# Routing on column tiles, paired output gates, and rows turned by one VectorE transpose and 16 DMAs

## The chip, the cores and the metric

The kernel runs on one core of a Trainium2 chip. The metric is the device time of one execution in microseconds (us). PE is TensorE (with its weight loads, PEld, beside the matmuls), DVE is VectorE, ACT is ScalarE, POOL is GpSimd, SP is SyncE, which issues most DMAs.

## The reference

Two Flamingo-like layers over 16 batches of 256 tokens of width 256, all in float32:

```python
x = x + tanh(g_xattn[0]) * L0_xattn(ctx, layernorm(x))          # 16 heads of 64, keys from ctx and x
x = x + tanh(g_ffn[0]) * L0_ffn(layernorm(x))                   # 8 experts, top 2 by softmax(x @ router_w.T)
x = x + tanh(g_xattn[1]) * L1_xattn(layernorm(x), ctx, ctx, ..) # 16 heads of 16, 77 keys
x = x + tanh(g_ffn[1]) * L1_ffn(layernorm(x), ..)               # gated linear attention, below

# L1_ffn: 8 heads of 64; q1, k1, v projections; a second pair q2, k2 of rank 64
# and a router over 4 experts (top 1)
o = gla(q1, k1, v, gk1) + sum over experts of gla(q2 * fac, k2 * fac, v, gk2 * mask)
g = (x @ Wga @ Wgb).reshape(B, L, H, DV)                         # the output gates, rank 64
o = o * rsqrt(mean(o * o) + EPS) * norm_w
o = o * (g * sigmoid(g))
return o.reshape(B, L, H * DV) @ Wo
```

The expert layer takes, of each token, the two most probable experts; a token's place among its expert's rows is the number of earlier tokens that chose that expert.

## The kernel before

The work is staged by layer, and each stage walks the 16 batches in a pipeline that is written out by hand. Nearly every instruction is pinned to program order on its engine, so each engine is a queue in the order of the code. A float32 matmul stands in the trace as two records.

**First stage (`stage0_fast`), cross-attention.** For each batch four units `g` of four heads: `scores` (PE `sc`), exponentials on ACT, `sums` on POOL, `values` (PE `o`, on four column tiles of 32), a DVE reciprocal and product. Between units stand tables of steps (`ahead_of`, `behind_scores`, `behind_values`), which also run the routing of the expert layer for earlier batches, in class `Route`: `logits` (after unit 3; PE `rt`: the turned rows `xnT` as weights, 128x128, and the 8 router columns as moving operand), `exps`, `choose`, `weigh`, `ranks` (after unit 2; PE `rank`: a strictly triangular matrix `before` and a matrix of ones as weights, 16 columns moving), `place`, and `scatter` by indirect DMA on POOL's queue. `copied` takes `rt` and `rank` from PSUM with ACT. The expert rows in DRAM are cleared first, by `clear_rows`: 16 DMAs of 640 KB on SP, from a zeroed tile of 128x256. The routing of the last two batches ends in the next stage, that of the experts.

**Last stage (`stage3_fast`), gated linear attention.** It runs 64 units `p`, four per batch `b` (step `p % 4` is `m`, two heads each). The loop over `p` does, in this order: `masked(p-1, 1)`, `keys_queries(p+1)` (PE `kq`), `middle`, `rest`, `decays(p+1)` (PE `gq`, `gz`; ACT exponentials `ee`), `late`, `products(p, 0)` (PE `sc<-f`), `masked(p, 0)` (DVE `at<-sc,amask`), `behind_mask`, `factors(p+1)`, `by_rows`, in steps 1 and 2 `summed(p)` (PE `o<-at,v`), `second(p+1)` (PE `gq`/`gz` from `low`), `factors_second(p+1)`, `logs`, `products(p, 1)` (PE `sc<-q,k`), and in steps 0 and 3 `summed(p)`. `middle`, `rest`, `late`, `behind_mask`, `by_rows` and `logs` are tables that give, for each step, functions and the batch that they work for (an offset to `b`).

The functions that the change touches: `lows` (step 0, next batch) makes the low-rank products `low`; its rows 0 to 63 of part 1 are the output gates' input. `outgates(b, i)` (steps 0 and 3) makes half of the gates: two matmuls on rows 0 to 63 into one PSUM bank `zg`, an exponential on ACT; `outgates_end` copies `zg` on DVE to `zs`, takes log and exponential on ACT and multiplies on POOL into `gw`. `gated` (steps 1 and 3) uses `gw`. For the batch after next, `stats` (step 2) takes the moments, `norm_ahead` (step 2) writes the normed rows `xn` with ACT, and `turn_ahead` (step 3) turns them with 16 DVE transposes of 32x128 (`turned_squares`). `route_logits` (step 0, next batch) transposes `low` on PE into a bank `rt`, which DVE then reads.

PSUM in the last stage: `psu` holds `kq`, `gq`, `gz`, `o` (one bank each), `psa` one pair of banks for `sc`, and the pool behind `bank(name)`, f3ps, has two banks that all other results take in turn: in step 0 `den`, `low`, `rt`, `zg`; in step 1 `z`, `z`, `ms`; in step 2 `hT`, `both`, `proj`; in step 3 `ms`, `v`, `v`, `zg`.

Of the kernel before, what the change touches and what calls it, by code (L numbers as in the profile page):

```python
# [10 lines left out]
F32 = mybir.dt.float32  # L11
I32 = mybir.dt.int32
AF = mybir.ActivationFunctionType
ALU = mybir.AluOpType
# [3 lines left out]
P = 128  # L18
# [55 lines left out]
def layers(ctx: ExitStack, tc: tile.TileContext, t, out, check):  # L74
# [67 lines left out]
    for b in range(2, B):  # L142
        load_x(b)
    rw1 = load_w("rw1", D, 8, ws1)
    ew1 = load_w("ew1", D, 2048, ws1)
# [3 lines left out]
    if fast:  # L149
        bv, own, pmask = (w12.tile(shape, F32, tag=n, name=n) for n, shape in (  # L150
            ("bv", [P, D]), ("own", [P, 2, 32]), ("pmask", [P, 2])))
        before, offs = (ws1.tile(shape, F32, tag=n, name=n) for n, shape in (
            ("before", [P, P]), ("offs", [P, 2, 2, 8])))

        gbo = const("gbo", [P, D])
        for n, x in (("bv", bv), ("bo", gbo), ("own", own), ("pmask", pmask), ("before", before),
                     ("offs", offs)):
            nc.sync.dma_start(out=x, in_=t[n])
    else:
        brow = w12.tile([1, 2, D], F32, tag="brow", name="brow")  # L160
        nc.sync.dma_start(out=brow, in_=t["brow"])
        bmask = w12.tile([P, 4], F32, tag="bmask", name="bmask")
        nc.sync.dma_start(out=bmask, in_=t["bmask"])
# [231 lines left out]
    class Route:  # L395
# [32 lines left out]
        def logits(self, b, bank):  # L428
            ps, xnT = bank("rt"), self.xnT.pop(b)
            for i in range(2):  # L430
                for k in range(2):
                    pe.matmul(ps[:, 8 * i:8 * i + 8], xnT[:, k, i * P:(i + 1) * P], rw1[:, k, :],
                              start=k == 0, stop=k == 1)
            self.copied(b, ps[:, :16])

        def copied(self, b, ps):
            n = ps.shape[1]
            self.ps[b] = ws1.tile([P, n], F32, tag=f"copied{n}", name="copied")
            act.copy(self.ps[b], ps)

        def exps(self, b):

            z = self.ps.pop(b)[:, :16].rearrange("p (i e) -> p i e", i=2)
            mx = st.tile([P, 2], F32, tag="rmx", name="rmx")
            dve.tensor_reduce(mx, z, AX.X, ALU.max)
            e = self.e[b] = st.tile([P, 2, 8], F32, tag="re", name="re")
            dve.tensor_tensor(e, z, bc(mx, [P, 2, 8], 2), ALU.subtract)
            act.activation(e, e, AF.Exp)
# [58 lines left out]
        def ranks(self, b, bank):  # L507
            hs, h1, h2 = self.hs[b]
            ps = bank("rank")
            pe.matmul(ps[:, :16], before, hs[:, 0].rearrange("p i e -> p (i e)"), start=True, stop=True)  # L510
            pe.matmul(ps[:, 16:32], ones, hs[:, 1].rearrange("p i e -> p (i e)"), start=True, stop=True)
            self.copied(b, ps[:, :32])

        def place(self, b):

            (_, h1, h2), ps, count = self.hs.pop(b), self.ps.pop(b), check["rows"][:, b // 8]
            base = st.tile([P, 2, 2, 8], F32, tag="base", name="base")
            at = st.tile([P, 2, 2, 2, 8], F32, tag="at", name="at")
            row = st.tile([P, 2, 2, 2], F32, tag="row", name="row")
            n = st.tile([P, 2, 8], F32, tag="nth", name="nth")  # L520
            dve.tensor_tensor(n, ps[:, :16].rearrange("p (i e) -> p i e", i=2), bc(count, [P, 2, 8], 1), ALU.add)
            dve.tensor_tensor(count, count, ps[:, 24:32], ALU.add)
            dve.tensor_tensor(n[:, 1, :], n[:, 1, :], ps[:, 16:24], ALU.add)
            dve.tensor_tensor(base[:, 0], n, offs[:, 0], ALU.add)

            dve.scalar_tensor_tensor(base[:, 1], n, ROWS - 1.0, offs[:, 1], ALU.min, ALU.add)
            for k, h in enumerate((h1, h2)):
                dve.tensor_tensor(at[:, :, :, k], base, bc(h, [P, 2, 2, 8], 1), ALU.mult)
            dve.tensor_reduce(row, at, AX.X, ALU.add)
            dve.tensor_copy(self.pos[:, b], row)  # L530
# [24 lines left out]
    def clear_rows():  # L555
        zero = ws1.tile([P, D], F32, tag="zero", name="zero")
        nc.gpsimd.memset(zero, 0.0)
        n = ROWS // P
        for rows in route.rows:
            for e in range(8):  # L560
                nc.sync.dma_start(out=by_expert(rows, e),
                                  in_=bc(zero, [P, n, D], 1))

# [341 lines left out]
    def stage1():  # L905
        with ExitStack() as sx:
# [7 lines left out]
            def route(b):  # L914
# [4 lines left out]
                for i in range(2):  # L919
                    for k in range(2):  # L920
                        nc.tensor.matmul(ps[:, 8 * i:8 * i + 8], xnT[:, k, i * P:(i + 1) * P], rw1[:, k, :],
                                         start=k == 0, stop=k == 1)
# [694 lines left out]
    def stage3_fast(early_bank):  # L1617

        with ExitStack() as sx:
# [22 lines left out]

            lbg2 = w1.tile([64, 512], F32, tag="lbg2", name="lbg2")
            nc.sync.dma_start(out=lbg2, in_=t["lbg"][64:P, :])
            low2 = w1.tile([64, P], F32, tag="low2", name="low2")
# [3 lines left out]

            xn, xnT, low, lg, hT, em, am = {}, {}, {}, {}, {}, {}, {}  # L1650
            v, gw, u_, oT = {}, {}, {}, {}
# [17 lines left out]
            def norm_ahead(b):  # L1669
                xn[b] = w0.tile([P, 2, D], F32, tag="xn", name="xn")  # L1670
                normed(xn[b], xs[b], *mvs.pop(b))

# [8 lines left out]
            def turn_ahead(b):  # L1681

                xnT[b] = of(b).tile([P, 2, S], F32, tag="xnT", name="xnT")
                turned_squares(xnT[b], xn[b], range(16))

            def lows(b):
# [7 lines left out]
                dve3.tensor_copy(low[b][:, 0, :], ps[:, :S])  # L1694
                dve3.tensor_scalar(low[b][:, 1, :], ps[:, S:], vec[:, V_ONE:V_ONE + 1], None, ALU.add)
                if b > 0:
                    for r in range(0, 64, 32):
# [95 lines left out]

            def outgates(b, i):

                if i == 0:
                    gw[b] = w2.tile([P, 4, S], F32, tag="gw", name="gw")
                ps = bank("zg")
                for m in range(2):
                    matmul(ps[:, m * S:(m + 1) * S], lbg[0:64, (2 * i + m) * P:(2 * i + m + 1) * P],  # L1800
                           low[b][0:64, 1, :], start=True, stop=True)
                e = w2.tile([P, 512], F32, tag="eg", name="eg")
                act3.activation(e, ps, AF.Exp, scale=-1.0)
                z_[b, i] = ps, e

            def outgates_end(b, i):
                ps, e = z_.pop((b, i))
                zs = w2.tile([P, 512], F32, tag="zs", name="zs")
                dve3.tensor_copy(zs, ps)
                act3.activation(e, e, AF.Ln, bias=1.0)  # L1810
                act3.activation(e, e, AF.Exp, scale=-1.0)
                pool3.tensor_tensor(gw[b][:, 2 * i:2 * i + 2, :].rearrange("p m s -> p (m s)"), zs, e, ALU.mult)

# [121 lines left out]
            def squares(b, mp):  # L1935
                if mp == 0:
                    u_[b] = w2.tile([P, 4, S], F32, tag="u", name="u")
                    oT[b] = w2.tile([P, 4, S], F32, tag="oT", name="oT")
                ps = o.pop((b, mp))
# [44 lines left out]
            def warm():  # L1984

                ps = bank("warm")
                for _ in range(2):
# [6 lines left out]

            rest = {0: [(bias, 2)], 1: [(route, 1)], 2: [(steepest, 1, 0), (stats, 2)], 3: [(steepest, 1, 1), (turn_ahead, 2)]}
            late = {1: [(scaled, -1, 1)], 2: [(project, -1)], 3: [(vals, 1)]}
            behind_mask = {0: [(route_logits, 1)]}
            by_rows = {0: [(outgates, 0, 0)], 1: [(gates_end, 1)], 3: [(outgates, 0, 1)]}
            logs = {0: [(route_sums, 1), (outgates_end, 0, 0)], 1: [(gate_logs, 1, 0)], 2: [(gate_logs, 1, 1), (norm_ahead, 2)],
                    3: [(outgates_end, 0, 1)]}  # L2000

# [138 lines left out]
def _arrays(i):  # L2140
# [4 lines left out]
    def cols(v):  # L2145
# [34 lines left out]
        "wo0h": f["L0_xattn_Wo"].reshape(4, 4, 2, 32, D).transpose(0, 2, 1, 3, 4).reshape(1024, D),  # L2180
        "rw1": f["L0_ffn_router_w"].T, "ew1": f["L0_ffn_expert_weights"].transpose(1, 0, 2).reshape(D, 2048),
        "prio": np.broadcast_to(np.arange(8, 0, -1, dtype=np.float32), (P, 8)),
# [3 lines left out]
        "wq3": f["L1_ffn_Wq"], "wk3": f["L1_ffn_Wk"], "wv3": f["L1_ffn_Wv"], "wo3": f["L1_ffn_Wo"],  # L2186
        "before": (s < u) * np.float32(1),
        "offs": np.broadcast_to(np.float32([ALL_ROWS, ROWS]).reshape(2, 1, 1) * np.arange(8, dtype=np.float32), (P, 2, 2, 8)), "smask": smask, "halves": halves.astype(np.float32),
# [18 lines left out]
```

## Time and profile before

| | |
|---|---|
| median of 3 runs | 1860.68 us (1860.09 to 1863.35) |
| the profiled execution | 1860.41 us, span 1858.6 us |
| granted TensorE clock | 0.998 |
| PE, DVE, POOL, ACT busy | 99%, 66%, 55%, 46% |
| first stage (`sc`, `o`, `qk`, most of `rt` and `rank`) | to about 933 us |
| gated linear attention | from about 1213 us, in steady state from 1242 us |

In the lines below L50 is the helper that issues pinned instructions and L1635 and L1638 are the last stage's matmul and transpose helpers, so groups are told apart by the names of the tiles: `zg<-low,lbg` writes `zg` from `low` and `lbg`. A timeline's line gives start and duration in us, engine, line, operation, tiles, shape and count; in brackets the idle time before it and what ended it.

### The profile page before, as it was taken

The numbers are of one execution on the slowest core, as the hardware profiler recorded it, in microseconds if no ns is written. First come the engines' busy times: TensorE is split into PE (matmuls) and PEld (weight loads), VectorE is DVE, ScalarE is ACT, GpSimd is POOL, SyncE is SP. The second block draws the span as 40 slices with busy tenths as digits, with TensorE's granted clock in tenths as the row PEclk, the third lists the DMA queues.
The fourth block names the chain that finished last, engine by engine and source line by source line (L and its number), as shares of the span: only waits on it lengthen the run. The fifth ranks groups of instructions, "written<-read, shape, count | busy, mean of one in ns | idle before, by whom it ended". The sixth has DMA issues, their size and how long they took to land.

```text
span 1858.6 us, 34765 instructions
## 1 busy us (share of the span) xinstructions
PE 1833.0 (99%) x13678; PEld 1270.8 (68%) x13678; DVE 1231.4 (66%) x2903; ACT 863.9 (46%) x1804; POOL 1016.0 (55%) x1001
## 2 busy tenths in 40 slices
PE   8999999999999999999999999999999999999997
PEld 5666666666766667666777766667777777777775
DVE  3345656556655656555465388878888888888874
ACT  4433344343443434434343487845544545454542
POOL 4654767567666576656634767314444444444443
PEclk9999999999999999999999999999999999999999
DMA  9500010000010000000068933100000000000000
GB/s 322 204 3 20 18 32 15 25 16 22 24 37 7 29 20 10 28 24 19 10 213 249 250 50 48 18 1 1 12 7 7 7 12 7 7 7 7 13 7 14
DMA packets 56902, 84.62 MB, mean 46 GB/s; under 512 B 10467, under 2 KB 44371, under 8 KB 56217
## 3 DMA queue, kind: packets, MB, share of 16 engines
q1 hardware_dynamic: 44441, 65.52, 10.7%
q0 software_dynamic: 12288, 16.79, 4.5%
q8 instruction: 110, 1.80, 0.4%
q14 instruction: 63, 0.52, 0.1%
HBM read 44.00 MB, written 38.29 MB: 44 GB/s over the span
## 4 chain that ended last, share of the span: by engine, by line
PE 94%; DVE 2%; ACT 1%; POOL 1%; issue 1%; DMA 0%; SPq 0%; POOLq 0%; DVEq 0%; ACTq 0%
PE o L50 14%; PE qk L50 13%; PE sc L50 11%; PE v L50 9%; PE proj L50 7%; PE kq L1635 7%; PE sc L1635 5%; PE gq L1635 3%; PE ex L50 3%; PE v L1635 3%; PE proj L1635 3%; PE o L1635 3%; PE gz L1635 2%; PE low L1635 1%; PE ms L1635 1%; PE q L50 1%
## 5 line engine op out<-in xcount | busy, mean ns | idle before, releaser
L50 POOL TENSOR_SCALAR rs<-mv 128x2 f32<-128x2 f32 (+2 forms) x85 | 16.2, 191 | 395.4 <-DVE mv L50 393.2
L50 DVE RECIPROCAL rd<-o 128x256 f32<-128x256 f32 x64 | 112.4, 1756 | 162.6 <-PE o L50 162.6
L50 ACT ACTIVATE e<-sc 128x1024 f32<-128x1024 f32 (+1 forms) x192 | 181.5, 1015 | 18.5 <-PE sc L50 18.5
L50 PE MATMUL sc<-qk 64*128 64x256 f32 (+1 forms) x1536 | 183.1, 384 | 0.5 <-DVE qk L50 0.5
L50 PE MATMUL o<-e,v 128*32 128x256 f32 (+1 forms) x3072 | 177.9, 379 | 0.0
L50 PEld LDWEIGHTS sc<-qk 64*128 64x128 f32 (+1 forms) x1536 | 132.1, 172 | 55.0 <-issue 26.8
L50 POOL TENSOR_TENSOR esum<-esum,es 128x512 f32<-128x512 f32 x128 | 163.2, 1275 | 10.0
L50 PE MATMUL qk<-kvT,wkv 128*128 128x333 f32 x512 | 164.3, 443 | 0.0
L50 POOL TENSOR_TENSOR es<-e 128x1024 f32<-128x1024 f32 x64 | 151.2, 2363 | 13.7 <-ACT e L50 10.6
L50 POOL TENSOR_TENSOR at<-at,at 128x768 f32<-128x768 f32 x63 | 114.0, 1809 | 74.5 <-DVE at L50 73.6
L50 ACT ACTIVATE qk<-qk 128x256 f32<-128x256 f32 x128 | 48.9, 382 | 227.1 <-PE qk L50 227.1
L50 POOL TENSOR_TENSOR es<-es,e 77x1024 f32<-77x1024 f32 x64 | 150.3, 2348 | 5.0
L50 PEld LDWEIGHTS o<-e,v 128*32 128x32 f32 (+1 forms) x3072 | 99.8, 110 | 66.4
L50 DVE COPY qk<-qk 128x333 f32<-128x333 f32 x128 | 64.6, 505 | 106.8 <-ACT qk L50 104.9
L50 PE MATMUL qk<-kvT,wq 128*128 128x256 f32 x512 | 134.4, 385 | 0.0
L50 POOL DMA_INDIRECT x<-rows_out,pos x64 | 100.9, 1577 | 34.7 <-issue 17.2
L50 PEld LDWEIGHTS qk<-kvT,wkv 128*128 128x128 f32 x512 | 97.2, 190 | 30.0
L50 PEld LDWEIGHTS qk<-kvT,wq 128*128 128x128 f32 x512 | 94.4, 189 | 33.7 <-issue 13.7
L50 PE MATMUL proj<-wo0h,oT 128*128 128x256 f32 x512 | 113.5, 380 | 0.0
L50 PE MATMUL v<-wkv,kvT 128*128 128x512 f32 x256 | 113.0, 594 | 0.0
L50 POOL TENSOR_TENSOR gw<-zs,eg 128x512 f32<-128x512 f32 x32 | 40.7, 1273 | 120.5 <-ACT eg L50 115.8
L50 PEld LDWEIGHTS proj<-wo0h,oT 128*128 128x128 f32 x512 | 96.0, 190 | 13.3 <-issue 0.8
(261 smaller groups left out, 4124.4 us busy)
## 6 DMA issues: line engine op xcount, KB each, us to landing
rows<-zero SPq DMA_DIRECT2D x16, 640.0 KB
xin<-rows SPq DMA_DIRECT2D x16, 640.0 KB
rows_out<-y SPq DMA_DIRECT2D x16, 384.0 KB
v<-vctx SPq DMA_DIRECT2D x15, 308.0 KB
x<-in_x_dram SPq DMA_DIRECT2D x16, 256.0 KB
rows_out<-y SPq DMA_DIRECT2D x16, 256.0 KB
out_dram<-x SPq DMA_DIRECT2D x15, 256.0 KB
wkv<-in_wkv_dram SPq DMA_DIRECT2D x2, 1024.0 KB
```

The lines of the kernel that those rows point to most:

```text
L50: x = getattr(self.engine, name)(*a, **k)
L1635: tc.keep_in_program_order(nc.tensor.matmul(*a, **k))
```

## The change

Routing: the 32 (padded) router columns become the weights, on four column tiles of 32, and the turned rows move, 64 columns (32 tokens of each half) per tile; one DVE transpose of 128x64 in squares of 32x32 (`turned`) takes the place of ACT's copy. `ranks` does the same with the choices `hs` as weights. The cleared rows come from a zero tile of 128x128, so each piece of the DMA is 512 B instead of 1024 B.

Last stage: all output gates of a batch are made in step 0, in pairs, on rows 0 to 63 and 64 to 127, into two banks. The second half's operands are a copy of the gate weights (`lbg2`) and of `low` (`lowd`, by one DMA). ACT copies `zs`. `outgates_end` runs in steps 0 and 1. `stats` moves from step 2 to step 1, `norm_ahead` from step 2 to step 1, `turn_ahead` from step 3 to step 2. `norm_ahead` writes its rows in another order of columns, and `turn_ahead` is one DVE transpose of 128x512 and 16 DMAs from SBUF to SBUF, which place the squares.

```diff
-    rw1 = load_w("rw1", D, 8, ws1)
+    rw1 = load_w("rw1", D, 32, ws1)
...
         def logits(self, b, bank):
             ps, xnT = bank("rt"), self.xnT.pop(b)
-            for i in range(2):
-                for k in range(2):
-                    pe.matmul(ps[:, 8 * i:8 * i + 8], xnT[:, k, i * P:(i + 1) * P], rw1[:, k, :],
+            for k in range(2):
+                for q in range(4):
+                    pe.matmul(ps[32 * q:32 * q + 32, :64], rw1[:, k, :],
+                              xnT[:, k, :].rearrange("p (i q t) -> p i q t", i=2, q=4)[:, :, q, :],
                               start=k == 0, stop=k == 1)
-            self.copied(b, ps[:, :16])
+            self.turned(b, ps)
+        def turned(self, b, ps):
+            self.ps[b] = ws1.tile([P, 2, 32], F32, tag="turned", name="turned")
+            dve.transpose(self.ps[b].rearrange("p n e -> p (n e)"), ps[:, :64])
...
         def ranks(self, b, bank):
-            pe.matmul(ps[:, :16], before, hs[:, 0].rearrange("p i e -> p (i e)"), start=True, stop=True)
-            pe.matmul(ps[:, 16:32], ones, hs[:, 1].rearrange("p i e -> p (i e)"), start=True, stop=True)
-            self.copied(b, ps[:, :32])
+            for q in range(4):
+                pe.matmul(ps[32 * q:32 * q + 32, :64], hs.rearrange("p w i e -> p (w i e)"),
+                          before[:, q:5:4 - q, :], start=True, stop=True)
+            self.turned(b, ps)
...
-        zero = ws1.tile([P, D], F32, tag="zero", name="zero")
+        zero = ws1.tile([P, P], F32, tag="zero", name="zero")
...
-            lbg2 = w1.tile([64, 512], F32, tag="lbg2", name="lbg2")
-            nc.sync.dma_start(out=lbg2, in_=t["lbg"][64:P, :])
+            lbg2 = w1.tile([P, 512], F32, tag="lbg2", name="lbg2")
+            nc.sync.dma_start(out=lbg2[:64], in_=t["lbg"][64:P, :])
+            nc.sync.dma_start(out=lbg2[64:], in_=t["lbg"][:64, :])
...
             def norm_ahead(b):
-                normed(xn[b], xs[b], *mvs.pop(b))
+                every = "p i (k d) -> p i k d"
+                normed(xn[b].rearrange("p k (i d) -> p i k d", i=2), xs[b].rearrange(every, k=2), *mvs.pop(b))
...
             def turn_ahead(b):
                 xnT[b] = of(b).tile([P, 2, S], F32, tag="xnT", name="xnT")
-                turned_squares(xnT[b], xn[b], range(16))
+                y = w1.tile([P, 4, P], F32, tag="turned", name="turned")
+                dve3.transpose(y.rearrange("p x d -> p (x d)"), xn[b].rearrange("p k d -> p (k d)"))
+                to = xnT[b].rearrange("p k (i s) -> p (k i) s", i=2)
+                for q in range(0, P, 32):
+                    for r in range(0, P, 32):
+                        nc.sync.dma_start(out=to[r:r + 32, :, q:q + 32], in_=y[q:q + 32, :, r:r + 32])
...
             def lows(b):
+                lowd[b] = of(b).tile([P, S], F32, tag="lowd", name="lowd")
+                nc.sync.dma_start(out=lowd[b][64:], in_=low[b][:64, 1, :])
...
-            def outgates(b, i):
-                if i == 0:
-                    gw[b] = w2.tile([P, 4, S], F32, tag="gw", name="gw")
-                ps = bank("zg")
-                for m in range(2):
-                    matmul(ps[:, m * S:(m + 1) * S], lbg[0:64, (2 * i + m) * P:(2 * i + m + 1) * P],
-                           low[b][0:64, 1, :], start=True, stop=True)
-                e = w2.tile([P, 512], F32, tag="eg", name="eg")
-                act3.activation(e, ps, AF.Exp, scale=-1.0)
-                z_[b, i] = ps, e
+            def outgates(b):
+                gw[b] = w2.tile([P, 4, S], F32, tag="gw", name="gw")
+                two = [bank("zg"), bank("zg")]
+                for i in range(2):
+                    for h, (w, x) in enumerate(((lbg[0:64], low[b][0:64, 1, :]), (lbg2[64:], lowd[b][64:]))):
+                        m = 2 * i + h
+                        matmul(two[h][:, i * S:(i + 1) * S], w[:, m * P:(m + 1) * P], x, start=True, stop=True)
+                for h, ps in enumerate(two):
+                    e, zs = (w2.tile([P, 512], F32, tag=n, name=n) for n in ("eg", "zs"))
+                    act3.activation(e, ps, AF.Exp, scale=-1.0)
+                    act3.copy(zs, ps)
+                    z_[b, h] = zs, e
...
-                zs = w2.tile([P, 512], F32, tag="zs", name="zs")
-                dve3.tensor_copy(zs, ps)
...
-            rest = {0: [(bias, 2)], 1: [(route, 1)], 2: [(steepest, 1, 0), (stats, 2)], 3: [(steepest, 1, 1), (turn_ahead, 2)]}
+            rest = {0: [(bias, 2)], 1: [(route, 1), (stats, 2)], 2: [(turn_ahead, 2), (steepest, 1, 0)], 3: [(steepest, 1, 1)]}
-            by_rows = {0: [(outgates, 0, 0)], 1: [(gates_end, 1)], 3: [(outgates, 0, 1)]}
-            logs = {0: [(route_sums, 1), (outgates_end, 0, 0)], 1: [(gate_logs, 1, 0)], 2: [(gate_logs, 1, 1), (norm_ahead, 2)],
-                    3: [(outgates_end, 0, 1)]}
+            by_rows = {0: [(outgates, 0)], 1: [(gates_end, 1)]}
+            logs = {0: [(route_sums, 1), (outgates_end, 0, 0)], 1: [(norm_ahead, 2), (outgates_end, 0, 1), (gate_logs, 1, 0)], 2: [(gate_logs, 1, 1)]}
```

`oT` also takes the buffer of `u_` (a place in SBUF saved), `before` gets 32 columns of ones beside its 128, and `place` and `exps` read the new layout.

More of the change, by code (lines that the diff above doesn't have):

```diff
@@ L152, in layers @@
         before, offs = (ws1.tile(shape, F32, tag=n, name=n) for n, shape in (
-            ("before", [P, P]), ("offs", [P, 2, 2, 8])))
+            ("before", [P, 5, 32]), ("offs", [P, 2, 2, 8])))
         gbo = const("gbo", [P, D])
@@ L429, in logits @@
             ps, xnT = bank("rt"), self.xnT.pop(b)
-            for i in range(2):
-                for k in range(2):
-                    pe.matmul(ps[:, 8 * i:8 * i + 8], xnT[:, k, i * P:(i + 1) * P], rw1[:, k, :],
+            for k in range(2):
+                for q in range(4):
+                    pe.matmul(ps[32 * q:32 * q + 32, :64], rw1[:, k, :],
+                              xnT[:, k, :].rearrange("p (i q t) -> p i q t", i=2, q=4)[:, :, q, :],
                               start=k == 0, stop=k == 1)
-            self.copied(b, ps[:, :16])
[L436 to L439, printed above, removed]
+            self.turned(b, ps)
+        def turned(self, b, ps):
+            self.ps[b] = ws1.tile([P, 2, 32], F32, tag="turned", name="turned")
+            dve.transpose(self.ps[b].rearrange("p n e -> p (n e)"), ps[:, :64])
         def exps(self, b):
-            z = self.ps.pop(b)[:, :16].rearrange("p (i e) -> p i e", i=2)
+            z = self.ps.pop(b)[:, :, :8]
             mx = st.tile([P, 2], F32, tag="rmx", name="rmx")
@@ L520, in place @@
             n = st.tile([P, 2, 8], F32, tag="nth", name="nth")
-            dve.tensor_tensor(n, ps[:, :16].rearrange("p (i e) -> p i e", i=2), bc(count, [P, 2, 8], 1), ALU.add)
-            dve.tensor_tensor(count, count, ps[:, 24:32], ALU.add)
-            dve.tensor_tensor(n[:, 1, :], n[:, 1, :], ps[:, 16:24], ALU.add)
+            dve.tensor_tensor(n, ps[:, 0, :16].rearrange("p (i e) -> p i e", i=2), bc(count, [P, 2, 8], 1), ALU.add)
+            dve.tensor_tensor(count, count, ps[:, 1, 24:32], ALU.add)
+            dve.tensor_tensor(n[:, 1, :], n[:, 1, :], ps[:, 1, 16:24], ALU.add)
             dve.tensor_tensor(base[:, 0], n, offs[:, 0], ALU.add)
@@ L560, in clear_rows @@
             for e in range(8):
-                nc.sync.dma_start(out=by_expert(rows, e),
-                                  in_=bc(zero, [P, n, D], 1))
+                nc.sync.dma_start(out=by_expert(rows, e).rearrange("p n (x d) -> p (n x) d", d=P),
+                                  in_=bc(zero, [P, 2 * n, P], 1))
     def stage0_fast():
@@ L920, in route @@
                     for k in range(2):
-                        nc.tensor.matmul(ps[:, 8 * i:8 * i + 8], xnT[:, k, i * P:(i + 1) * P], rw1[:, k, :],
+                        nc.tensor.matmul(ps[:, 8 * i:8 * i + 8], xnT[:, k, i * P:(i + 1) * P], rw1[:, k, :8],
                                          start=k == 0, stop=k == 1)
@@ L1648, in stage3_fast @@
             hots = [w1.tile([P, 2, 4], F32, tag=f"hot{n}", name=f"hot{n}") for n in range(2)]
-            xn, xnT, low, lg, hT, em, am = {}, {}, {}, {}, {}, {}, {}
+            xn, xnT, low, lg, hT, em, am, lowd = {}, {}, {}, {}, {}, {}, {}, {}
             v, gw, u_, oT = {}, {}, {}, {}
@@ L1792, in vals, with outgates_end @@
                     act3.copy(v[b][:, i, :], ps)
-            def outgates(b, i):
-                if i == 0:
-                    gw[b] = w2.tile([P, 4, S], F32, tag="gw", name="gw")
-                ps = bank("zg")
-                for m in range(2):
-                    matmul(ps[:, m * S:(m + 1) * S], lbg[0:64, (2 * i + m) * P:(2 * i + m + 1) * P],
-                           low[b][0:64, 1, :], start=True, stop=True)
-                e = w2.tile([P, 512], F32, tag="eg", name="eg")
-                act3.activation(e, ps, AF.Exp, scale=-1.0)
-                z_[b, i] = ps, e
-            def outgates_end(b, i):
-                ps, e = z_.pop((b, i))
-                zs = w2.tile([P, 512], F32, tag="zs", name="zs")
-                dve3.tensor_copy(zs, ps)
+            def outgates(b):
[10 more added lines that the diff above has]
+                    z_[b, h] = zs, e
+            def outgates_end(b, h):
+                zs, e = z_.pop((b, h))
                 act3.activation(e, e, AF.Ln, bias=1.0)
                 act3.activation(e, e, AF.Exp, scale=-1.0)
-                pool3.tensor_tensor(gw[b][:, 2 * i:2 * i + 2, :].rearrange("p m s -> p (m s)"), zs, e, ALU.mult)
+                pool3.tensor_tensor(gw[b][:, h::2, :], *(x.rearrange("p (m s) -> p m s", m=2) for x in (zs, e)), ALU.mult)
             def place(p):
@@ L1937, in squares @@
                     u_[b] = w2.tile([P, 4, S], F32, tag="u", name="u")
-                    oT[b] = w2.tile([P, 4, S], F32, tag="oT", name="oT")
+                    oT[b] = u_[b]
                 ps = o.pop((b, mp))
@@ L2180, in _arrays @@
         "wo0h": f["L0_xattn_Wo"].reshape(4, 4, 2, 32, D).transpose(0, 2, 1, 3, 4).reshape(1024, D),
-        "rw1": f["L0_ffn_router_w"].T, "ew1": f["L0_ffn_expert_weights"].transpose(1, 0, 2).reshape(D, 2048),
+        "rw1": np.concatenate([f["L0_ffn_router_w"].T, z((D, 24), np.float32)], axis=1), "ew1": f["L0_ffn_expert_weights"].transpose(1, 0, 2).reshape(D, 2048),
         "prio": np.broadcast_to(np.arange(8, 0, -1, dtype=np.float32), (P, 8)),
@@ L2186, in _arrays @@
         "wq3": f["L1_ffn_Wq"], "wk3": f["L1_ffn_Wk"], "wv3": f["L1_ffn_Wv"], "wo3": f["L1_ffn_Wo"],
-        "before": (s < u) * np.float32(1),
+        "before": np.concatenate([(s < u) * np.float32(1), np.ones((P, 32), np.float32)], axis=1).reshape(P, 5, 32),
         "offs": np.broadcast_to(np.float32([ALL_ROWS, ROWS]).reshape(2, 1, 1) * np.arange(8, dtype=np.float32), (P, 2, 2, 8)), "smask": smask, "halves": halves.astype(np.float32),
```

## The prediction

> **What bounds the kernel now.** I read the page's parts 1 and 4 first, then the busy time by stretches, then the timeline of one batch of the last stage and of one routing step of the first.
>
> ```profile
> PE 1833.0 (99%) x13678; PEld 1270.8 (68%) x13678; DVE 1231.4 (66%) x2903; ACT 863.9 (46%) x1804; POOL 1016.0 (55%) x1001
> ...
> PE 94%; DVE 2%; ACT 1%; POOL 1%; issue 1%; DMA 0%; SPq 0%; POOLq 0%; DVEq 0%; ACTq 0%
> ```
>
> (Busy time and share of each engine; the chain of waits by engine.) Of a stretch of the last stage:
>
> ```profile
> 1400.00:1600.00 200.00, 200.00 (x1284) 145.30 (x1282) 168.10 (x400) 102.43 (x234) 94.07 (x95) 1.00 0.02 8
> ```
>
> (Busy time, and count in brackets, of PE, weight loads, DVE, ACT, POOL; then PE clock, DMA share, GB/s.) The chain is PE work, and in the last stage PE is busy 200.00 of 200 us. But a matmul's record overlaps the next one's, so this does not say what PE waits for; DVE has 168 of 200 there. Whether freed PE time is a gain is read from one batch, engine by engine.
>
> ```profile
> 1472.06 0.92 PE L1635 MATMUL sc<-f 64*128 64x256 f32 x8
> 1472.83 0.28 PE L1638 MATMUL rt<-ident,low 64*128 64x64 f32 x2
> 1472.90 0.91 PE L1635 MATMUL zg<-low,lbg 64*128 64x256 f32 x3
> ...
> 1474.21 0.92 PE L1635 MATMUL sc<-q,k 64*128 64x256 f32 x8
> ...
> 1501.22 0.92 PE L1635 MATMUL sc<-f 64*128 64x256 f32 x8
> ```
>
> (PE; start, duration.) Step 3 of a batch has its `sc<-f` at 1463.08 and the next batch at 1501.22: 38.14 us a batch. In every step `sc<-f` and `sc<-q,k` share one PSUM buffer (`psa`, bufs=1), and between them VectorE must empty it (`masked`):
>
> ```profile
> 1473.10 0.96 DVE L50 TENSOR_TENSOR at<-sc,amask 128x768 f32<-128x768 f32 x1 [0.26 <-PE rt L1638]
> 1473.98 0.15 DVE L50 TENSOR_REDUCE emx<-rt 128x2 f32<-128x8 f32 x1
> 1474.17 0.17 DVE L50 TENSOR_TENSOR e<-rt,emx 128x8 f32<-128x8 f32 x1
> ```
>
> The distance from `sc<-f` to `sc<-q,k` is 2.15 us in step 0, 2.19 in step 1 (1480.80, 1482.99) and step 2 (1491.17, 1493.36), 2.22 in step 3 (1463.08, 1465.30), though PE does different work in each. VectorE alone accounts for it: it starts 1.04 after `sc<-f`, takes 0.96, and the weight load behind it about 0.15: 2.15. The matmuls put in between fill this wait and are nearly free.
>
> **The change, part by part.**
>
> *Output gates, step 3.* `zg` leaves step 3. What is left between the products is `gq`/`gz`, 0.53 us as in step 1 (1482.46 to 1482.99). PE then has 0.85 + 0.53 = 1.38 us of work against VectorE's 2.15 and waits 0.77. The sixteen 32x128 transposes (16 x 0.302, ending at 1464.16) no longer stand ahead of `masked`, so the distance falls from 2.22 to 2.15-2.17. Gain 0.05 x 15 batches = 0.8 us, not the 0.9 us a batch that `zg` occupied.
>
> *Output gates, step 0.* Four gate matmuls instead of two, in pairs on rows 0-63 and 64-127. Each is two records of 256 columns, 0.216 us each (kq: 16 records of 256 columns, 216 ns from start to start). Before, rows 0-63 carry 4 `zg` and 2 `gq` records: 6 x 0.216 = 1.30, from 1472.90 to 1474.21, as seen. After, each half carries 4 `zg` and 2 of `gq` or `gz`: again 1.30. So the pairing fits all gates into the old time, if it can start. It can't: `outgates` now takes two banks at once, and the pool `bank` (f3ps) has two. Before `outgates` step 0 takes `den`, `low`, `rt`; the first `zg` reuses the bank of `low` (free by 1472.85), the second that of `rt`, which is free only when VectorE has read it, behind `masked`: 1474.17 + 0.17 = 1474.34, which is 2.28 after `sc<-f`. Add 0.15 for the release and the weight load: 2.43. From there rows 64-127 need their six records: 2.43 + 1.30 = 3.73 for `sc<-q,k`, against 2.15 now. Loss 1.58 us in each batch that has a `rt` (15): **+23.7 us**. Behind the waiting PE stand `gq`/`gz`, the second products, the values and the next step; nothing later in the batch has a PE wait that could give it back. Bounds: 1.15 (if `gq`/`gz` ran ahead: only the four zg slots, 0.86, after 2.43, so 3.3) to 1.9 (a second wait of the size of the `sc` load).
>
> The Trainium skill, TensorEngine Tiling (Array Packing), Restrictions and Gotchas, says that row tiling raises PSUM pressure because row tiles must write different banks. By that page's speed-up of up to 2x for a contraction of 64 or less alone, the last stage would win about 0.9 x 16 = 14 us, an estimate. The trace bears out the first rule, in that `zg` already waits for a bank (that of `low`, read until 1472.85), and has no run of the second.
>
> *VectorE, step 1.* Removed: two `zs` copies (0.68) and 16 transposes (4.84) a batch; added: one 128x512 transpose, between 0.44 (`dens`, 128x256) and 4.84, taken as 2 x 0.44 = 0.88. `stats` (0.74 + 0.30 at 1488.67) moves from step 2 into the 1.00 us that VectorE waits in step 1 before `masked`, so it just fits. But the two-operand small operations of `route` stall while POOL works:
>
> ```profile
> 1477.93 1.72 DVE L50 TENSOR_TENSOR e<-e,eden 128x8 f32<-128x8 f32 x1
> ```
>
> (0.17 unhindered; POOL runs its 1.80 us `at` from 1477.82.) After the change `gw` (1.27) and `at` (1.80) follow each other on POOL from about 6.65 us after step 0's `sc<-f`, to 9.7; `route` then ends near 10.7 and `stats` near 11.5, while step 1's `sc<-f` (8.74 now, 10.32 later) wants `masked` at 11.36. I take +0.15 x 15 = **+2.2 us**; bounds 0 and 0.5 x 15 = 7.
>
> *ScalarE.* Two more 0.59 copies in step 0, one `eg` there instead of in step 3. From `eg` at 3.1 it runs 0.58 x 4, then 0.38, 1.29, 0.58 and is done at 7.1; `lg<-z` starts at 8.46. Hidden by 1.3 us; if that is gone, each us late is a us of `psa`.
>
> *The turned rows.* Sixteen DMAs on SP a batch, 0.3-0.45 us to issue each (7 us), after the transpose near 1488; landing takes 2.5 us (median of `rows<-xw`). They are there by 1498, and `lows` reads at 1469.35 + 38.14 = 1507.5. Hidden by 9 us; uncovered, up to 10 us x 14 batches. Behind them on SP stand only `out` and `lowd`, for which nobody waits within a batch. The 2048 packets of 128 B take 13 ns each in this trace: 2048 x 13 / 16 = 1.7 us of the DMA engines. The Trainium skill (DMA: Bandwidth & Descriptors, Specifications) wants 512 B for line rate; at the trace's 27 ns for such a packet it would be 3.5 us, hidden all the same.
>
> *Routing on column tiles (first stage).*
>
> ```profile
> 123.74 2.56 PE L50 MATMUL o<-e,v 128*32 128x256 f32 x44
> 126.23 1.06 PE L50 MATMUL rt<-rw,rxnT 128*128 128x8 f32 x8
> 127.14 1.11 PE L50 MATMUL qk<-kvT,wq 128*128 128x256 f32 x4
> ```
>
> Here PE runs without gaps. `qk` starts 0.84 after `o`'s end (126.30); without `rt` in between it starts 0.07 before it (68.86 + 2.78, 71.57). So `rt` costs 0.91: eight loads of 128 columns for 8-column matmuls. `rank`: 165.48 - 165.09 + 0.07 = 0.46. After: 16 and 8 records of 64 columns on four column tiles, as `o<-e,v` runs them: (2.56 - 0.38) / 10 = 0.218 for four of 256 columns, so 0.054 for four of 64; 4 x 0.054 = 0.22 and 2 x 0.054 = 0.11. Gain 0.69 + 0.35 = 1.04, x 14 = **-14.6 us**. If the four tiles didn't overlap, 16 x 0.054 = 0.86 would leave 0.8 us in all; `o<-e,v` is the same form, so I take 1.04. One `rt` and two `rank` lie in the next stage (up to 1.4, where DMA is 90% busy): 0.7. Transposes of 128x64 (at most 0.44 each) replace ScalarE copies (0.17, 0.19); VectorE is 60% busy there (119 of 200) and hides them, 14 us at most if not.
>
> *Cleared rows.* 20480 packets of 512 B (27 ns) instead of 10240 of 1024 B (46): 34.6 instead of 29.4 us of the DMA engines. SP's issue then ends 5 us later, and so does the second batch's `v` load (70.13), which PE reads at 88.7. Free; at twice the clearing time it would cost 10 us once. The wider `rw1` and `before`, the second half of `lbg2` and `oT` in `u`'s buffer (two batches deep, as now) add a load of 128 KB and no wait on the path.
>
> Sum: -14.6 - 0.7 - 0.8 + 23.7 + 2.2 = +9.8. The profiled execution took 1860.41 (span 1858.6), within 0.02% of the median 1860.68; 1860.4 + 9.8 = **1870**.
>
> **Rivals.** (a) No wait for `rt`'s bank (another placing of the banks, or VectorE reads it early): step 0 keeps 2.15, and the sum is -14.6 - 0.7 - 0.8 = -16: 1845. For it: first-stage gain is the same. Against: three live tiles, two banks. (b) The wait comes and VectorE is late in step 1 by 0.5-1 us: +5 to +13 more, 1875-1883. It decides once `route` and `stats` end later than 11.36. For it: every `e<-e,eden` of the trace but one waited out a POOL operation. (c) The wait comes, but the first stage wins little, since column tiles or VectorE don't keep up: 1884. (d) The wait is the short one (1.15) and routing gains fully: 1860.4 - 16.1 + 17.3 + 1 = 1862.6, no change.
>
> **How the numbers follow.** A measurement of this kernel can tell about 0.2% (3.7 us). Forecast 0.62 (own range 1864-1877), (a) 0.12, (b) 0.14, (c) 0.05, (d) 0.07. Faster 0.12 is (a); same 0.11 is (d) and 0.04 of the forecast's low edge; slower 0.77 is the rest. The range 1857 to 1884 leaves out (a) and a little of (b) and (c).
>
> **What would show it.** Right: in step 0 the second `zg` starts about 2.4 after `sc<-f`, behind VectorE's `e<-rt`; `sc<-q,k` stands 3.7 after it in step 0 and still 2.15 in step 3; the batch takes about 39.7 us; the first stage's batch is about 1 us shorter (56.0 or 59.7 between `rt`s now). Wrong: a batch at or under 38.1, a gate matmul that doesn't wait, or `low` waiting for a DMA.

## The result and the profile after

The changed kernel takes 1871.99 us (median of 9 runs, 1870.05 to 1881.38), the kernel before beside it 1860.83 us (9 runs, 1859.95 to 1864.41): a ratio of 1.0062, 95% interval 1.0046 to 1.0078. It is 11 us slower; 1870 was forecast.

The profiled execution of after took 1876.16 us (span 1874.3), 4.2 us above the median: the granted TensorE clock fell in two places, ahead of the last stage's steady part. Between the last expert matmul and the first `sc<-f` of the last stage this profile loses 5.6 us, most of it there (1050.01 to 1241.24, against 1061.42 to 1247.00 before), so differences are taken within a stage. Two windows of after (busy time and count of PE, weight loads, DVE, ACT, POOL; then PE clock, DMA share, GB/s), one with a clock of 0.66 and one of the steady stretch:

```profile
1210.00:1215.00 5.00, 4.38 (x24) 3.08 (x28) 4.46 (x5) 1.95 (x4) 0.00 (x0) 0.66 0.01 3
...
1400.00:1600.00 200.00, 190.93 (x1234) 138.22 (x1232) 134.29 (x299) 103.36 (x234) 88.86 (x90) 1.00 0.07 16
```

The second line answers to the 200.00 of PE and 168.10 of DVE before: VectorE has lost 34 us of work in 200, and PE now has gaps of 9 us. The page's parts 1 and 4 say the same of the whole:

```profile
PE 1819.4 (97%) x13870; PEld 1255.3 (67%) x13870; DVE 1177.5 (63%) x2693; ACT 876.9 (47%) x1804; POOL 1016.9 (54%) x1001
...
PE 83%; POOL 7%; DVE 5%; ACT 2%; issue 2%; DMA 1%; POOLq 0%; SPq 0%; DVEq 0%; ACTq 0%
```

PE's work fell by 14 us and the time rose. The chain, 94% PE before, now runs through POOL (7%) and DVE (5%): new waits for both. Where the time went, by the start of the same instructions in both traces:

| | before | after | difference |
|---|---|---|---|
| last `sc` of the first stage | 929.28 | 917.88 | -11.4 |
| last expert matmul of the next stage | 1061.42 | 1050.01 | -11.4 |
| a batch of the last stage | 38.13 | 39.63 | +1.50, 15 times: +22.5 |
| of it, step 0, 1, 2, 3 | 8.74, 10.37, 10.05, 8.97 | 10.28, 10.40, 10.05, 8.91 | +1.54, +0.03, 0, -0.06 |

-11.4 + 22.5 = +11.1, the measured difference. (Two of after's batches took 39.98.) Before, `o<-at,v` of step 0 starts 3.00 after `sc<-f` (1472.06):

```profile
1475.06 0.87 PE L1635 MATMUL o<-at,v 128*64 128x256 f32 x8
```

Step 0 of a batch of after, in the timeline (in brackets the idle time ahead and what ended it; the helpers of L1635 and L1638 stand at L1637 and L1640 in after):

```profile
1515.56 0.92 PE L1637 MATMUL sc<-f 64*128 64x256 f32 x8
...
1516.39 0.70 PE L1637 MATMUL zg<-low,lbg 64*128 64x256 f32 x2
1516.60 0.96 DVE L50 TENSOR_TENSOR at<-sc,amask 128x768 f32<-128x768 f32 x1 [0.26 <-PE rt L1640]
...
1517.66 0.17 DVE L50 TENSOR_TENSOR e<-rt,emx 128x8 f32<-128x8 f32 x1
...
1517.97 0.45 PE L1637 MATMUL zg<-lowd,lbg 64*128 64x256 f32 x1 [0.89 <-DVE e L50]
...
1519.16 0.99 PE L1637 MATMUL sc<-q,k 64*128 64x256 f32 x7
...
1520.09 0.87 PE L1637 MATMUL o<-at,v 128*64 128x256 f32 x8
```

The first bank's first matmul (two records) starts at once. The second bank's (`zg<-lowd`) waits until VectorE has done `masked` (`at<-sc,amask`) and then read `rt`: 2.41 after `sc<-f`. All that stands behind it on PE follows from there, and `o<-at,v` stands 4.53 after `sc<-f` instead of 3.00. Step 3 just ahead of it, which lost its gates:

```profile
1506.65 0.92 PE L1637 MATMUL sc<-f 64*128 64x256 f32 x8
...
1507.69 0.96 DVE L50 TENSOR_TENSOR at<-sc,amask 128x768 f32<-128x768 f32 x1 [4.92 <-PE sc L1637]
...
1508.79 0.92 PE L1637 MATMUL sc<-q,k 64*128 64x256 f32 x8 [0.79 <-DVE at L50]
```

PE has nothing left to do ahead of the second products and waits 0.79 us for VectorE: `sc<-q,k` still stands 2.14 after `sc<-f`.

### The profile page after: what moved, and what is told of

The parts are those of the page before. It is cut to its first block, busy times and chain, and to the rows that moved or that the text cites. A ratio compares the mean times of both kernels' runs of the same rounds, so it can differ in the third digit from the quotient of the medians.

```text
span 1874.3 us, 35312 instructions
## 1 busy us (share of the span) xinstructions
PE 1819.4 (97%) x13870; PEld 1255.3 (67%) x13870; DVE 1177.5 (63%) x2693; ACT 876.9 (47%) x1804; POOL 1016.9 (54%) x1001
## 4 chain that ended last, share of the span: by engine, by line
PE 83%; POOL 7%; DVE 5%; ACT 2%; issue 2%; DMA 1%; POOLq 0%; SPq 0%; DVEq 0%; ACTq 0%
PE o L50 11%; PE qk L50 11%; PE v L50 9%; PE sc L50 8%; PE proj L50 7%; PE kq L1637 6%; PE sc L1637 5%; POOL es L50 4%; PE gq L1637 3%; PE v L1637 3%; PE proj L1637 3%; PE o L1637 3%; PE ex L50 3%; PE gz L1637 2%; DVE at L50 2%
## 5 line engine op out<-in xcount | busy, mean ns | idle before, releaser
L50 DVE TENSOR_TENSOR at<-sc,amask 128x768 f32<-128x768 f32 x64 | 60.8, 950 | 86.4 <-PE sc L1637 71.8
```

The source lines that it names most:

```text
L50: x = getattr(self.engine, name)(*a, **k)
```

## The experiments

The theory: (1) the routing gains in the first stage, (2) the second gate bank waits in step 0 for VectorE's read of `rt`, (3) what is taken out of step 3, on PE or on VectorE, gains nothing, because PE's queue and `masked` already filled the same 2.15 us. Ratios below are to the kernel before, timed on the same chip (its medians 1863.37, 1860.12 and 1862.29 in the three sets).

| run | median us | ratio | 95% interval |
|---|---|---|---|
| routing alone | 1850.19 | 0.9931 | 0.9919 to 0.9944 |
| no gates in step 3 | 1864.00 | 1.0002 | 0.9990 to 1.0013 |
| turned rows alone | 1861.29 | 0.9992 | 0.9983 to 1.0001 |
| after, `rt` in `gq`'s bank | 1861.21 | 0.9986 | 0.9977 to 0.9996 |
| after, `rt` later | 1849.64 | 0.9943 | 0.9930 to 0.9956 |
| after, values moved in step 3 | 1858.10 | 0.9987 | 0.9979 to 0.9996 |
| before, values moved in step 3 | 1858.23 | 0.9987 | 0.9977 to 0.9997 |
| after, both edits | 1841.60 | 0.9888 | 0.9873 to 0.9903 |
| routing alone, no `esum` | 1846.32 | 0.9918 | 0.9904 to 0.9932 |
| both edits, `esum` shared | 1838.43 | 0.9878 | 0.9862 to 0.9893 |

**One part alone.** The kernel before with the hunks of `logits`, `turned`, `ranks`, `place`, `exps` and `clear_rows` only:

> The kernel before with the routing part alone (logits and ranks on column tiles, their VectorE transposes, the zero tile of 128x128); the last stage is that of before. My theory: the routing is worth what the trace of after shows up to the last stage, -11 us, so 1849 to 1850, and the last stage keeps 38.13 a batch. The prediction's own size was -15.3: 1845.5. Rival (the gain of the first stage is given back in the expert stage, which is fed by DMA): 1857 to 1861.

Measured 1850.19, with 38.14 a batch in the last stage and -11.5 at the last `sc` of the first. So the routing is a gain of 0.7%, smaller than forecast, and the other two parts together cost some 22 us (1871.99 - 1850.19; 24 by the two ratios).

The kernel before with the turned rows only (`norm_ahead`, `turn_ahead`, their steps, `oT`):

> The kernel before with the turned rows alone: one VectorE transpose of 128x512 and 16 DMAs in place of 16 transposes, stats and norm_ahead in step 1, turn_ahead in step 2, oT in the buffer of u; gates and routing are those of before. My theory: the 4.14 us of VectorE that it frees are not on the path but for the 0.05 to 0.07 of step 3, so -1 us, 1858.5 to 1861. Rival A (VectorE bounds the last stage as a whole): 4.1 x 14 = -58, 1803. Rival B (the rows come late, since the 16 issues take 11.3 us on SP): PE waits in lows, up to +5 us a batch, over 1870.

Measured 1861.29, no difference that can be told; 38.07 a batch, step 3 at 8.91 instead of 8.97. Over 4 us of VectorE a batch were worth 0.06. The 16 DMAs cost nothing either, with less to spare than forecast; SP's issues in the timeline of after (SPq is SP's queue):

```profile
1493.73 11.27 SPq L1693 DMA_DIRECT2D xnT<-turned  x16
```

That is 0.70 us each, not 0.3 to 0.45 (10.25 to 11.42 us for the 16 in the other batches). The issues end at 1505.0, and `low<-xnT,la` reads the rows at 1512.85 without a wait.

**Freed PE time in step 3.**

```diff
-                ps = bank("zg")
-                for m in range(2):
+                ps = bank("zg") if i == 0 else v[b][:, 0, :]
+                for m in range(2 if i == 0 else 0):
```

> The kernel before without the two gate matmuls (four records, 0.9 us of PE) of step 3: ACT and VectorE read the tile v in place of the bank zg, so half of the gates are not computed. My theory (VectorE's 1.04 + 0.96 + 0.15 between sc<-f and sc<-q,k sets the distance, and PE work put in between is free): the distance in step 3 stays at 2.15 to 2.22 and the time at 1859 to 1861. Rival (PE, busy 200 of 200 us, is the bound of the last stage): 0.9 x 16 = 14 us less, 1846.

Measured 1864.00 against 1863.37. Step 3 before, and in that run:

```profile
1463.08 0.92 PE L1635 MATMUL sc<-f 64*128 64x256 f32 x8
...
1465.30 0.92 PE L1635 MATMUL sc<-q,k 64*128 64x256 f32 x8
```

```profile
1468.38 0.92 PE L1635 MATMUL sc<-f 64*128 64x256 f32 x8
...
1470.60 0.92 PE L1635 MATMUL sc<-q,k 64*128 64x256 f32 x8 [0.86 <-DVE at L50]
```

The distance is 2.22 in both, with 0.9 us of PE work less in the second; the work has become a wait of 0.86. "PE 200.00 of 200" was no evidence that PE time could be won there.

**The wait for rt's bank.** First attempt, `rt` in a bank that is not one of the two:

```diff
-                ps = bank("rt")
+                ps = gq[4 * b - 3] if b > 0 else bank("rt")
```

> The kernel after, with rt written to the free half of the bank gq of the next unit instead of one of the two banks in turn; nothing else changes. My theory (the second zg bank is rt's, which VectorE frees only behind masked): the second zg no longer waits for VectorE; in step 0 the distance from sc<-f to o<-at,v falls from 4.53 back to about 3.0, the batch from 39.63 to 38.1, the whole by 15 x 1.53 = 23 us, from 1872 to about 1849. Rival A (the gates in step 0 are late for another reason: the copy lowd, or four more gate records on PE): the batch stays at 39.6 and the time at 1872. Rival B (a second wait stands right behind it, such as VectorE behind the POOL port in step 1): the batch ends between, 38.6 to 39.2, 1857 to 1866.

Measured 1861.21 and 38.87 a batch: half of what I expected, the case of rival B. The timeline shows the first wait gone and its successor:

```profile
1465.13 0.92 PE L1637 MATMUL sc<-f 64*128 64x256 f32 x8
...
1466.01 0.43 PE L1637 MATMUL zg<-lowd,lbg 64*128 64x256 f32 x1
...
1467.23 0.17 DVE L50 TENSOR_TENSOR e<-gq,emx 128x8 f32<-128x8 f32 x1
...
1467.45 0.48 PE L1637 MATMUL gq<-low,lbk 64*128 64x256 f32 x1 [0.36 <-DVE e L50]
```

`zg<-lowd` starts 0.88 after `sc<-f`. But `gq<-low,lbk` writes the other half of the bank in which VectorE reads `rt`, and it waits for that read: `o<-at,v` comes 3.61 after `sc<-f`, and step 1 is 0.17 longer, since VectorE, 0.9 us nearer to the step before, ends `stats` late. The Trainium skill (PSUM — Partial Sum Buffer, PSUM bank collisions raise a hardware error) says to guard PSUM by bank and quadrant, since another address of the same bank and quadrant collides too; the wait in this row is what that rule asks for.

Second attempt: `rt` behind everything else of step 0, when nobody waits for its bank, and `stats` in VectorE's idle time of step 1. `rt_made` and `rt_read` are the two halves of `route_logits`, its transposes and VectorE's reads (`emx`, `e`); `behind_sums` runs after `summed(p)`:

```diff
-            copies = {2: [(turned_hot, 1)]}
+            copies = {1: [(rt_read, 1), (stats, 2)], 2: [(turned_hot, 1)]}
...
-            rest = {0: [(bias, 2)], 1: [(route, 1), (stats, 2)], ...
+            rest = {0: [(bias, 2)], 1: [(route_sums, 1), (route, 1)], ...
...
-            behind_mask = {0: [(route_logits, 1)]}
+            behind_mask = {}
+            behind_sums = {0: [(rt_made, 1)]}
...
-            logs = {0: [(route_sums, 1), (outgates_end, 0, 0)], ...
+            logs = {0: [(outgates_end, 0, 0)], ...
```

> The kernel after with the transposes rt moved to the end of step 0, behind o<-at,v, in the bank that the first gates leave, and their VectorE reads, the sums behind them and stats moved into step 1 (stats into VectorE's 1.15 us wait for sq). So both zg banks are free early, and nothing else has to be read behind masked. The run with rt in gq's bank had the first wait gone (second zg 0.98 after sc<-f) and a new one in its place: gq<-low,lbk waits for e<-gq (same bank), 0.7 us a batch, and step 1 was 0.17 longer. My theory: step 0's o<-at,v at about 3.0 after sc<-f, 0.2 for rt at its end, step 1 back at 10.37; batch 38.3 instead of 39.63, 20 us less than after: 1852. Rival (all the gates in step 0 need over 2.15 us of PE, wherever rt stands): o<-at,v at 3.5 or later, batch 38.8 or more, 1859 or more.

Measured 1849.64 and 38.33 a batch, steps 9.01, 10.37, 10.05, 8.91.

```profile
1465.16 0.92 PE L1637 MATMUL sc<-f 64*128 64x256 f32 x8
...
1466.00 0.48 PE L1637 MATMUL zg<-lowd,lbg 64*128 64x256 f32 x1
...
1467.31 0.92 PE L1637 MATMUL sc<-q,k 64*128 64x256 f32 x8
...
1468.96 0.33 PE L1640 MATMUL rt<-ident,low 64*128 64x64 f32 x2
```

`sc<-q,k` is back at 2.15 after `sc<-f` with all four gates in between: the eight gate records of both halves take the room that four took before. `o<-at,v` is back at 3.00, so the bank was the whole of the wait. Of step 0's 1.54 us, 1.27 are gone; the 0.27 that remain are `rt`, now outside the wait.

**Putting work into step 3's wait.** One number decides where `summed` stands:

```diff
-                inside = p % 4 in (1, 2) and p + 1 < last
+                inside = p % 4 in (1, 2, 3) and p + 1 < last
```

> The kernel after with o<-at,v of step 3 put between the two products, as in steps 1 and 2 (one number in a condition). My theory: with the gates gone from step 3, PE waits 0.77 us there for VectorE's masked; 0.8 us of other PE work put into that wait is free, so step 3 falls from 8.91 to 8.15 and the whole by 0.77 x 16 = 12 us, to 1860. Rival A (PE is busy all the time, and moving work is no gain): 1872. Rival B (at of the unit before is not summed by POOL yet, and o waits): slower than 1872.

Measured 1858.10; step 3 of the batch:

```profile
1455.67 0.92 PE L1637 MATMUL sc<-f 64*128 64x256 f32 x8
1456.52 0.87 PE L1637 MATMUL o<-at,v 128*64 128x256 f32 x8
...
1457.86 0.82 PE L1637 MATMUL sc<-q,k 64*128 64x256 f32 x8
```

`o<-at,v` fits into the wait, `sc<-q,k` stands at 2.19 (2.14 without it), and the step falls from 8.91 to 8.05. The control is the same edit in the kernel before, where the gates are still in step 3:

> The kernel before with o<-at,v of step 3 put between the products, the same number in the same condition, with the gates still in step 3. My theory: the wait of 2.15 for masked is already filled there by zg and gq/gz (sc<-f 0.85 and 1.30 of others), so the 0.8 us of o put into it only push sc<-q,k to about 3.0, and step 3 stays at 8.97; 1859 to 1862. Rival (o between the products is a gain by itself, and the pairing has nothing to do with it): step 3 at 8.1 to 8.2, 1848.

Measured 1858.23, ratio 0.9987; step 3 at 8.91:

```profile
1465.92 0.92 PE L1635 MATMUL sc<-f 64*128 64x256 f32 x8
...
1467.63 0.87 PE L1635 MATMUL o<-at,v 128*64 128x256 f32 x8
...
1468.97 0.82 PE L1635 MATMUL sc<-q,k 64*128 64x256 f32 x8
```

There `o` only pushes `sc<-q,k` from 2.21 to 3.05. The move pays 0.86 us a batch where the gates have left and 0.06 where they haven't. Both edits of after together:

> The kernel after with both edits: rt at the end of step 0, and o<-at,v of step 3 between the products. My theory: the two are independent (steps 0 and 3), so 20 + 12 = 32 us less than after, a batch of 37.5, 1840; 10 us under the routing alone, which is what pairing the gates could have given. Rival (VectorE or POOL becomes the bound of the shorter batch): 37.8 or more, over 1845.

Measured 1841.60 and 37.47 a batch (steps 9.01, 10.37, 10.05, 8.05). The change of the last stage with these edits is worth having, 0.66 us a batch against 38.13: step 3 is 0.92 shorter and step 0 0.27 longer. So the gates' new place pays once the bank is free and something is put into the hole that they leave. The same moves with unpaired gates were not run, so the share of the pairing itself is not shown. PE is full again:

```profile
1400.00:1600.00 200.00, 200.00 (x1294) 146.67 (x1294) 142.26 (x309) 106.63 (x245) 94.53 (x95) 1.00 0.08 17
```

**Why the first stage gained 11.4 and not 14.6.** By the shift of the matmuls between the two traces, `ranks` gains 0.33 in every batch, as forecast (0.35). `logits` gains 0.67 (forecast 0.69), but in 6 of 14 batches 0.3 of it is lost again by the next `rank`, and once all of it: 14 x 1.00 - 6 x 0.30 - 0.67 = 11.5. In the place followed here it is lost at an `o<-es,ones`. This place in before and in the routing alone:

```profile
316.88 2.34 POOL L50 TENSOR_TENSOR es<-es,e 77x1024 f32<-77x1024 f32 x1
...
319.69 0.64 PE L50 MATMUL o<-es,ones 128*32 128x256 f32 x8
```

```profile
314.66 2.35 POOL L50 TENSOR_TENSOR es<-es,e 77x1024 f32<-77x1024 f32 x1
...
317.06 0.64 PE L50 MATMUL o<-es,ones 128*32 128x256 f32 x8 [0.22 <-POOL es L50]
```

Before, POOL's sum ended 0.47 ahead of the matmul that reads it (319.22, 319.69); now PE has come nearer and waits. In the routing alone POOL works almost without a gap (0.2 at most) from 301.75 to 319.76 (`es`, `es`, `esum` twice, `rs`, the issue of `rows`, and `es`, `es`, `esum` again), so it can't follow. To test it I left `esum` out:

> The routing alone, without POOL's two additions esum<-esum,es in each unit of the first stage (the check sum of the exponentials is left out). In the routing alone o<-es,ones waits for POOL's es in some batches, and of rt's 0.67 us the batch gets only 0.36 there. My theory (POOL's sums had only 0.4 us to spare and now end last): the wait goes, the first stage gains about 0.3 us in 9 of 14 batches, some 2.5 to 3 us, and its last sc stands 14 us earlier than in before instead of 11.6; 1847. Rival (the VectorE transposes of 128x64 hold up ScalarE's exponentials): the first stage stays at -11.6, 1850. The 5.3 us of POOL a unit are many times that wait, so more than 14.6 would mean that POOL held the first stage before the change too.

Measured 1846.32; the last `sc` of the first stage stands 13.6 earlier than in before, the last expert matmul 13.8. The waits of PE between 130 and 920 us (total us, times, longest), the routing alone and then without `esum`:

```profile
PE o L50 <- POOL es L50: 2.1, 8, 0.4
```

```profile
PE o L50 <- POOL es L50: 0.4, 1, 0.4
```

`logits` now gains its 0.67 in 13 of the 14 batches and 0.37 in the one that still waits. VectorE's 128x64 transposes, the rival, are all still there. A version that leaves nothing out lets VectorE add half of the columns:

```diff
-                    pool.tensor_tensor(esum, esum, es[:, n, :], ALU.add)
+                    pool.tensor_tensor(esum[:, :S], esum[:, :S], es[:, n, :S], ALU.add)
...
+                for n in range(2):     # in values
+                    dve.tensor_tensor(esum[:, S:], esum[:, S:], es[:, n, S:], ALU.add)
```

> The run with both edits, and in the first stage VectorE adds half of the columns of the check sum esum, in values ahead of its reciprocal, where it waits 2 to 4.8 us for PE's o; POOL adds the other half (128x256 instead of 128x512, twice a unit). Nothing is left out. My theory (POOL's sums held o<-es,ones in the routing alone; without esum the first stage gained 2 us more): POOL is relieved of about 1.2 us a unit, the wait goes, the last sc of the first stage stands 13.5 us earlier than in before instead of 11.6, 1839 to 1840. Rival (VectorE's two-operand additions wait out POOL's operations and come late themselves): the first stage stays at -11.6 or less, 1842 or more.

Measured 1838.43, the lowest median of all; its interval overlaps that of the run with both edits, so by the times alone the two aren't told apart. The traces tell them apart: the last `sc` stands 12.8 earlier than in before, 1.2 more than with both edits and less than the 13.5 I expected, and PE's waits for `es` are 0.6 us in 2 places, where both edits alone have 1.9 us in 8. POOL's `es` now waits for VectorE's half of `esum`, 6.1 us in 10 places, which may be what is missing from the 13.5; no run tests it.

## Why the prediction was right

The forecast was the sum -14.6 - 0.7 - 0.8 + 23.7 + 2.2 = +9.8; the measured terms are -11.4, 0, -0.9, +23.1 and +0.45, in sum +11.2. The mechanism of the largest term was right. That the sum came within 1.4 us is in part luck: the gains of the first two stages fell short by 3.9, and step 0 and step 1 cost 2.4 less than forecast.

- **Step 0, the term that decides.** The forecast put the second `zg` 2.43 after `sc<-f` and the loss at 1.58; the trace has 2.41 and 1.54. (`sc<-q,k` itself starts at 3.39, its other records from 3.60, not at 3.73, since records on rows 0 to 63 run ahead of the last `zg` on rows 64 to 127.) Reading it from the order of the banks and from VectorE's queue (`masked`, `emx`, `e`) was enough, and the two attempts with `rt` confirm the cause. The short wait (rival d) and the absence of a wait (rival a) fell with it.
- **Step 3.** Forecast 0.05 a batch instead of PE's 0.9; measured 0.06. The run without gates and the run with the turn alone show both halves: the PE time that was freed there is worth nothing by itself, and the VectorE time 0.06.
- **First stage: mis-sized.** The working of the two terms held (0.69 and 0.35 forecast, 0.67 and 0.33 measured), but the step "here PE runs without gaps", that is, the whole gain counts in each batch, failed. At the place shown POOL was 0.47 from being late, and in half of the batches only 0.37 or nothing of the 0.67 came through. The rival with little first-stage gain named column tiles and VectorE as its causes; neither was. (Its price for tiles that don't overlap adds up to 1.1 us, 0.05 for `rt` and 0.03 for `rank` in 14 batches, not 0.8; the forecast doesn't use it.)
- **Next stage.** 0.7 was forecast for one `rt` and two `rank` there (two of each stand behind the last `sc`). In the profile of after the gain came and was lost again. Behind the last `rank` the matmuls stand 12.2 earlier than before, 0.8 more than the last `sc`; then the transposes of the expert rows wait for VectorE's copy `y`, which stands behind a reduction that waited for a DMA:

```profile
968.91 0.74 DVE L50 TENSOR_REDUCE mm<-mk 77x1 f32<-77x256 int32 x2 [2.34 <-DMA mk<-in_maskT_dram]
...
970.51 0.66 PE L50 MATMUL xT<-ident,xin 128*128 128x128 f32 x4 [0.56 <-DVE y L50]
```

In the profile of the routing alone that reduction waited 1.23 us, PE doesn't wait, and the last expert matmul starts at 1049.10, 12.3 earlier than before against 11.5 at the last `sc`: the 0.8 came through. Why the DMA came late in one profile and not in the other is open.

- **Step 1.** 0.15 a batch was forecast for VectorE being late; it was 0.03, because step 0 had become longer and gave VectorE the time. Where step 0 was short again (`rt` in `gq`'s bank) the lateness did appear, 0.17.
- **The turned rows.** One transpose of 128x512 takes 0.70, not 0.88; the issues take 11.3 us, not 7. Hidden all the same.
- **Row tiles.** The Trainium skill's rule (TensorEngine Tiling (Array Packing), Restrictions and Gotchas) that row tiling raises PSUM pressure, which the prediction weighed, was borne out as a price: 1.54 us a batch. The row of before that the prediction named for it doesn't show it: `zg` at 1472.90 has no idle time ahead. That page's speed-up for a contraction of 64 or less shows too: eight gate records in the place of four (`rt` later), though it counted only once other work filled the hole.

## What to carry to other kernels

An operation that takes two buffers of a pool of two waits for whoever read the last one, however short that read is: look for where the reader stands in its engine's queue. When PE work and a wait for another engine cover each other, taking one away gains nothing until the freed place is filled; look for the instruction that can be moved into it, and try the move with and without the change. And before a gain is counted in full, measure the distance to the engine that is next late: here it was 0.47 us at the place followed, less than the gain itself.

## What was not expected of the hardware

- A VectorE operation with two small operands in SBUF waits out a POOL operation also in the first stage: `re<-turned,rmx` took 0.72 in the routing alone, where POOL ran `es`, and 0.17 for `re<-copied,rmx` in before, where it fell between two POOL operations (at 308.77, as `es` ended). The Trainium skill (SBUF — State Buffer, SBUF: two separate sides) describes this as an exclusive lock of a shared port pair; the transposes and reductions beside it (0.24, 0.14) were not longer.
- A DMA of 32 partitions by four pieces of 128 B takes SP 0.64 to 0.71 us to issue (16 in 10.25 to 11.42 us in after).
- The granted TensorE clock can fall in the middle of an execution whose mean is 0.996: its mean was 0.66 between 1210 and 1215 us and 0.76 between 1228 and 1242 us of after. 5 x 0.34 + 14 x 0.24 = 5.1 us of PE's time, about what this profile stands above its median.
